# A graph network's second table kept by position: plain stores in place of scatters, and positions found ahead of the first table

## The chip, the core and the metric

The kernel runs on one core of one Trainium2 chip. The metric is the device time of one execution in microseconds (us), lower is better; the median of the runs is compared.

## What is computed

Two layers of a typed graph transformer over 6250 nodes of 128 features, 200000 edges sorted by destination, 32 relations (edge types) and 16 node types, then a dense layer and a normalised residual:

```python
def gt_layer(x, ntype, etype, src, dst, ...):        # 8 heads of 16
    k, q, v = (typed_linear(x, ntype, W) for W in (Wk, Wq, Wv))
    kT = jnp.einsum('nhd,htdo->nhto', k, Watt)       # one row per node and relation
    vT = jnp.einsum('nhd,htdo->nhto', v, Wmsg)
    kw, m = kT[src, :, etype], vT[src, :, etype]     # gathered per edge
    a = jnp.einsum('ehd,ehd->eh', kw, q[dst]) * pri[:, etype].T / SQRT_D
    att = edge_softmax(a, dst, n)
    hag = segment_sum((m * att[:, :, None]).reshape(-1, 128), dst, n)
    h = silu(typed_linear(hag, ntype, Wa))
    alpha = sigmoid(skip[ntype])[:, None]
    return layernorm(h * alpha + x * (1 - alpha)) * g + b
h = x
for l in range(2): h = gt_layer(h, ...)
return layernorm(x + (h @ ff_w + ff_b))
```

## The kernel before

The nodes are padded to 6272, 49 tiles of 128. For each layer a table in DRAM holds a row of 256 words (kT and vT, 1 KB) for every node and relation, 6272 x 32 rows, 205.5 MB. POOL then gathers, for each tile of 128 destinations, one row per edge and destination: a gather (line 887) is one indirect DMA that brings 128 rows, one per partition, into a slot of a ring of SBUF. There are 1613 gathers a layer. To keep that number small, destinations are sorted by their number of edges: a node's *position* is its place in that sorted list, tiles are made of neighbouring positions, and a tile takes as many slots as its largest destination has edges.

**First stretch.** Typed k and v columns are made by groups of two tiles (`one_typed`: masks on DVE at line 424, matmuls at 439), multiplied by the relations' weights (`table_rows`: matmul 472, emptied to one of four stages `sts` by ACT or DVE at 481), and sent to table 0 by SP (`send`, line 835, two DMAs of 1 MB for half a tile, 196 in all). The first three groups (`AHEAD`) come before a branch (`tc.If`) that would sort the edges if they weren't sorted. Beside this, `prepare` finds each destination's first edge with 50 gathers (535), its degree, and its position: a comparison with all bins (584, `hot`), counts by matmul (597 to 599, `total` and `ahead`), a running sum (602), a subtraction, an addition and a product (604 to 608), and a sum over bins (611, `pos_f`). From the positions follow `rec` (which node stands at a position), the x rows in order of position (663, 668) and the list `idx_all` of table rows by slot (673).

**Layer 0.** `gathers` issues on POOL; `attend` works on DVE with the slots that have landed, in pieces of up to 16 slots: product with the query (908), sum per head (910), softmax, product with the values (935), sum over slots (939). The rest of a group of tiles (four, at the end 3, 2, 2, 1, 1) runs in one *lane*: output map and norm (`behind`), then k and v of the next layer (`project`), then rows of table 1 (`next_tables`, again line 472 and 481) in two stages. A row of table 1 belongs to a node, tiles stand by position, so `scatter` (1129) writes each half tile, 2 MB, by an indirect DMA of POOL with the list `half`; 98 in all. A scatter stands in POOL's order among the gathers, `MARGIN` after its stage is planned to be full.

**Layer 1.** 1613 gathers from table 1 with the same `idx_all`, attention, and the output by 49 scatters.

**What sets the order.** Each engine runs its instructions in program order. The order is written by a planner: generators yield an engine, an estimated time and what they need, `plan.spawn` gives them a rank, and the planner emits the instruction that can start soonest by its estimates.

## Time and profile before

| what | us |
|---|---|
| median of 3 runs (lowest, highest) | 5355.41 (5348.28, 5358.69) |
| the profiled execution, its own time | 5361.82 |
| its span in the trace | 5360.0 |
| first stretch, to the first gather of layer 0 | 802.78 |
| layer 0, first to last gather | 802.78 to 3043.32 |
| layer 1, first gather | 3147.81 |
| busy: DVE, POOL, PE (TensorE matmul), ACT | 3876.2, 3552.9, 2562.4, 919.8 |

Times in rows are us from the start of the span unless marked ns. A row of windows gives the stretch, its length, the busy us (and count) of PE, PEld (weight loads), DVE, ACT and POOL, then TensorE's mean granted clock as a share of full speed, the share of time in which the 16 DMA engines were busy, and GB/s. In a timeline "[0.30 <-issue]" is the idle time of the engine ahead of the instruction and what ended it; "issue" is time in which it waited for nothing that the profile shows. A row of groups gives line, engine, operation, names out<-in, shapes and count, then the busy us and mean ns, then the idle time ahead of the group's instructions by what ended it. SPq is SP's queue: the us there is the time in which a DMA was being issued. DVE is VectorE, ACT ScalarE, POOL GpSimd, SP SyncE.

### The profile page before, as it was taken

The page shows a single profiled execution, that of the slowest core. Times are in us where ns is not written, and L with a number is a line of the kernel's source. Part 1 is how long each engine was busy: PE and PEld are TensorE (multiplying, and loading weights), DVE is VectorE, ACT ScalarE, POOL GpSimd, SP SyncE. Part 2 cuts the span into 40 slices and gives each one's busy share as a digit, 9 for nine tenths or more (in the row PEclk, how much of TensorE's full clock was granted, in tenths as well). Part 3 has the DMA queues.
Part 4 walks back from the last instruction along what each step waited for, and adds up shares of the span by engine and source line. Part 5 has one row for each costly group of instructions (what it writes and reads, how often), then busy time and mean ns, then how long its engine had stood idle before and what let it go on. Part 6 is the DMA issues. An engine that isn't in the chain of part 4 may idle for free. (4 is left out here: it accounts for less than half of the span.)

```text
span 5360.0 us, 35414 instructions
## 1 busy us (share of the span) xinstructions
PE 2562.4 (48%) x8598; PEld 1357.9 (25%) x8598; DVE 3876.2 (72%) x5522; ACT 919.8 (17%) x1814; POOL 3552.9 (66%) x3543
## 2 busy tenths in 40 slices
PE   6889972164755656565667841212213321221113
PEld 4455541022322322232334520101101111110002
DVE  5776755687787778777788826777777777776777
ACT  2233430011212211222223410000000000000001
POOL 0402306777777777777777547777777777777775
PEclk8899996576776667667777765656656655655556
DMA  6669985345646645655656643333333333333332
GB/s 243 261 250 390 365 330 129 106 151 179 207 142 206 221 146 186 223 196 183 203 198 240 239 167 114 108 115 114 116 106 114 115 110 105 112 110 108 109 102 76
DMA packets 323823, 923.80 MB, mean 172 GB/s; under 512 B 82896, under 2 KB 169932, under 8 KB 285976
## 3 DMA queue, kind: packets, MB, share of 16 engines
q0 software_dynamic: 176864, 645.82, 37.6%
q1 hardware_dynamic: 146744, 275.67, 14.2%
q8 instruction: 68, 1.11, 0.1%
q14 instruction: 147, 1.20, 0.1%
HBM read 488.51 MB, written 432.74 MB: 172 GB/s over the span
## 5 line engine op out<-in xcount | busy, mean ns | idle before, releaser
L887 POOL DMA_INDIRECT ring<-table,idx_all x3226 | 3240.8, 1005 | 1211.3 <-issue 970.0
L908 DVE TENSOR_TENSOR ring<-ring,sb 128x2048 f32<-128x2048 f32 (+13 forms) x261 | 453.8, 1739 | 728.1 <-DMA ring<-table,idx_all 709.1
L481 ACT COPY st<-tab 128x512 f32<-128x512 f32 x1175 | 614.2, 598 | 860.4 <-PE tab L472 437.7
L939 DVE TENSOR_REDUCE add<-ring 128x128 f32<-128x2048 f32 (+13 forms) x269 | 731.6, 2720 | 7.9
L1007 DVE SCALAR_TENSOR_TENSOR xm<-types,xb 128x512 f32<-128x512 f32 (+3 forms) x880 | 485.6, 588 | 103.5 <-PE av L1015 91.3
L472 PE MATMUL tab<-bv,vT 32*128 32x512 f32 x1568 | 405.1, 781 | 305.6 <-ACT st L481 303.9
L910 DVE TENSOR_REDUCE sb<-ring 128x128 f32<-128x2048 f32 (+13 forms) x269 | 472.9, 1758 | 7.0
L935 DVE TENSOR_TENSOR ring<-ring,sb 128x2048 f32<-128x2048 f32 (+13 forms) x269 | 469.4, 1745 | 0.0
L1015 PE MATMUL tab<-xm,wq 128*128 128x512 f32 (+3 forms) x416 | 215.6, 686 | 465.8 <-DVE xm L1007 465.8
L1015 PE MATMUL av<-xm,wa 128*128 128x512 f32 (+3 forms) x736 | 329.1, 610 | 201.5 <-DVE xm L1007 201.1
L481 DVE COPY st<-tab 128x512 f32<-128x512 f32 x393 | 256.3, 686 | 204.5 <-PE tab L472 137.3
L472 PE MATMUL tab<-bk,kT 32*128 32x512 f32 x1568 | 380.7, 780 | 25.4 <-ACT st L481 11.5
L1174 ACT COPY sb<-qr 128x128 f32<-128x128 f32 x96 | 25.9, 270 | 1849.9 <-DVE sb L910 1681.5
L1015 PE MATMUL av<-xm,wq 128*128 128x512 f32 (+3 forms) x544 | 237.2, 589 | 128.4 <-DVE xm L1007 126.3
L439 PE MATMUL kv<-xm,wk 128*128 128x256 f32 (+1 forms) x800 | 261.3, 409 | 63.1 <-DVE xm L424 63.0
L472 PEld LDWEIGHTS tab<-bv,vT 32*128 32x128 f32 x1568 | 174.2, 219 | 451.0 <-ACT st L481 401.6
L1015 PEld LDWEIGHTS av<-xm,wa 128*128 128x128 f32 x736 | 156.5, 230 | 369.2 <-DVE xm L1007 244.0
L1015 PEld LDWEIGHTS tab<-xm,wq 128*128 128x128 f32 x416 | 101.1, 269 | 568.3 <-DVE xm L1007 508.1
L439 PE MATMUL kv<-xm,wv 128*128 128x256 f32 (+1 forms) x800 | 243.2, 387 | 0.0
L1015 PE MATMUL ak<-xm,wk 128*128 128x512 f32 (+3 forms) x480 | 231.1, 566 | 24.8 <-DVE xm L1007 24.8
L1015 PE MATMUL av<-xm,wv 128*128 128x512 f32 (+3 forms) x480 | 222.0, 546 | 0.0
L1015 PE MATMUL tab<-xm,wa 128*128 128x512 f32 (+2 forms) x224 | 114.1, 672 | 178.6 <-DVE xm L1007 178.6
(207 smaller groups left out, 2917.1 us busy)
## 6 DMA issues: line engine op xcount, KB each, us to landing
table<-st SPq DMA_DIRECT2D x196, 1024.0 KB
ring<-table,idx_all POOLq DMA_INDIRECT x3226, 2.8
state<-init SPq DMA_DIRECT2D x2, 3528.0 KB
state<-state SPq DMA_DIRECT2D x98, 72.0 KB
types<-tyrow SPq DMA_DIRECT2D x20, 256.0 KB
rows<-in_x_dram SPq DMA_DIRECT2D x24, 128.0 KB
types_i<-in_node_type_dram SPq DMA_DIRECT2D x24, 128.0 KB
xperm<-xg SPq DMA_DIRECT2D x12, 256.0 KB
```

The costliest lines, as they stand in the source:

```text
L439: nc.tensor.matmul(to, w[:, t], xm, start=False, stop=last_of)
L472: nc.tensor.matmul(tab, cT[here, nodes], blk[here, t0 : t0 + per].rearrange("p t o -> p (t o)"), start=True, stop=True)
L481: (nc.scalar.copy if e == "ACT" else nc.vector.tensor_copy)(to, tab.rearrange("p (t o) -> p t o", o=width))
L887: nc.gpsimd.indirect_dma_start(out=ring[:, place], out_offset=None, in_=tables[layer], in_offset=bass.IndirectOffsetOnAxis(ap=idx[:, s : s ...
L908: nc.vector.tensor_tensor(kk, kk, q[:, None, :].to_broadcast([P, m, P]), op=ALU.mult)
L910: nc.vector.tensor_reduce(sc[:, s0 : s0 + m], kk.rearrange("p s (h d) -> p s h d", h=H), axis=AX.X, op=ALU.add)
L935: nc.vector.tensor_tensor(vv.rearrange("p s (h d) -> p s h d", h=H), vv.rearrange("p s (h d) -> p s h d", h=H), sc[:, s0 : s0 + m, :, None ...
L939: nc.vector.tensor_reduce(add, vv.rearrange("p s c -> p c s"), axis=AX.X, op=ALU.add)
L1007: nc.vector.scalar_tensor_tensor(xm[:, :M], types[:, :M], float(t), xT[:, :M], op0=ALU.is_equal, op1=ALU.mult)
L1015: nc.tensor.matmul(to[:, :M], w[:, t], xm[:, :M], start=(t == 0), stop=(t == NT - 1))
L1174: nc.scalar.copy(q, rows[0][:, j])
```

## The change

Table 1 is kept by position instead of by node. Its rows then lie in the order of the tiles, and SP stores each half tile by a plain DMA (`store`, line 1172 after); the list `half` and the scatters are gone. Layer 1 has to gather by position, so layer 0's table carries the place: its rows get a 257th word, 32 x position of the node + relation, added on DVE by `numbered`. In `attend` of layer 0, ACT copies that word of every landed slot over the slot's entry in `idx_all`. For that the positions must be known by node before any row of table 0 goes out: `pos_f` goes to DRAM (`posd`) and comes back turned, TensorE transposes it and DVE multiplies by 32 (`places`). So no table is made before the branch; typed columns run ahead and are kept for 11 groups (`KEPT`), the relations' weights are loaded late, the counts use five banks of PSUM instead of one, and the subtraction at 604 is folded into `upper`. A loop for more edges than slots, which runs no round with these edges, looks positions up by itself.

```diff
-AHEAD = 3
+AHEAD = 2
+KEPT = 11
+    WIDTH = [ROW + 1, ROW]
-    tables = [dtile(f"table{i}", [ROWS, ROW]) for i in range(L)]
+    tables = [dtile(f"table{i}", [ROWS, w]) for i, w in enumerate(WIDTH)]
+    posd = dtile("posd", [NP, 1])
...
+    def places(posn, got):
+        us = yield "PE", Work(P), [got]
+        to = tabs[0]
+        nc.tensor.transpose(to[:, :NTILE], posn, ident[:NTILE, :NTILE])
+        us = yield "DVE", 0.3, [us]
+        nc.vector.tensor_scalar(place32, to[:, :NTILE], float(RT), None, op0=ALU.mult)
+        known.us = us
...
-        nc.vector.tensor_scalar(upper, lanes, lane, None, op0=ALU.is_gt)
+        nc.vector.tensor_scalar(upper, lanes, lane, -1.0, op0=ALU.is_gt, op1=ALU.add)
+        counted = us
-                us = yield "PE", Work(112), [us]
-                n_ps = prep_bank()
+                us = yield "PE", Work(112), [counted]
+                n_ps = tabs[c0 // 448 % len(tabs)]
...
-        nc.vector.tensor_sub(upto, upto, total)
-        yield "DVE", dve_us(BT), ()
...
+        yield "SP", 0.4, [us]
+        nc.sync.dma_start(out=posd.rearrange("(p t) c -> p (t c)", t=NTILE), in_=pos_f)
+        got = yield "SP", 0.4, ()
+        posn = pp.tile([NTILE, P], F32, tag="posn")
+        nc.sync.dma_start(out=posn, in_=posd.rearrange("(t p) c -> t (p c)", p=P))
+        plan.spawn(places(posn, got + 5.0), RANK["prepare"])
...
-        if i > 1:
-            yield "SP", 0.0, [used[i - 2]]
-        kT, ks = yield from copied(ap, "kT", kv[:, :HALF], M, 2, [end])
+        if i >= KEPT:
+            yield "SP", 0.0, [used[i - KEPT]]
+        kT, ks = yield from copied(ap, "kT", kv[:, :HALF], M, KEPT, [end])
...
+    def relation_blocks():
+        us = yield "SP", 17.0, ()
+        relations.extend(load_relations(first, 0))
+        yield "DVE", 3.5, [us + 3.0]
+    def numbered(st, c, t, needs):
+        us = yield "DVE", 0.2, needs
+        nc.vector.tensor_scalar(st[:, :, ROW], kinds_r[:, c * RT // 2 :][:, : RT // 2], place32[:, t : t + 1], None, op0=ALU.add)
+        return us
     def first_tables(part):
+        yield "SP", 0.0, [known]
...
-        plan.spawn(first_tables(range(AHEAD)), RANK["table"], 8.0)
+        plan.spawn(relation_blocks(), RANK["late"], 25.0)
...
-        plan.spawn(first_tables(range(AHEAD, len(GROUPS))), RANK["table"])
+        plan.spawn(first_tables(range(len(GROUPS))), RANK["table"])
...
+            if after is not None:
+                done = yield "ACT", act_us(m), landed[s0 : s0 + m]
+                nc.scalar.copy(after[:, s0 : s0 + m], ring[:, r, ROW])
...
-    def scatter(t, c, rows, filled, done, margin, at):
-        us = yield "SP", 0.0, filled
-        us = yield "POOL", Issue(GATHER_US, STORE_US), [us + margin]
-        s = nc.gpsimd.indirect_dma_start(
-            out=tables[1].rearrange("(n t) c -> n (t c)", t=RT // 2),
-            out_offset=bass.IndirectOffsetOnAxis(ap=half[:, t, c : c + 1], axis=0), ...)
+    def store(t, c, rows, filled, done, at):
+        us = yield "SP", 0.8, filled
+        dest = tables[1][t * P * RT : (t + 1) * P * RT].rearrange("(p t) c -> p t c", t=RT)
+        nc.sync.dma_start(out=dest[:, c * RT // 2 :][:, : RT // 2], in_=rows)
```

POOL's order in layer 0, before, at one place (`table_60` is table 0, `table_61` table 1, `st` a stage; x9 is nine of them in a row):

```order
L1132 DMA table_61<-st_5709,half 12544x4096
L887 DMA ring<-table_60,idx_all 128x256 x9
L1132 DMA table_61<-st_5708,half 12544x4096
L887 DMA ring<-table_60,idx_all 128x256 x8
L1132 DMA table_61<-st_5709,half 12544x4096
L887 DMA ring<-table_60,idx_all 128x256 x8
L1132 DMA table_61<-st_5708,half 12544x4096
L887 DMA ring<-table_60,idx_all 128x256 x9
L1132 DMA table_61<-st_5709,half 12544x4096
```

And POOL's order after, from the last instruction of the first stretch's own (the branches between are the loop that runs no round) through layer 0:

```order
L914 DMA ring<-table_60,wi 128x257 x16
L998 REGISTER_ALU
L998 COMPARE_AND_BRANCH
L998 UNCONDITIONAL_BRANCH
L996 REGISTER_ALU
L996 COMPARE_AND_BRANCH
L996 UNCONDITIONAL_BRANCH
L914 DMA ring<-table_60,idx_all 128x257 x1613
L994 TENSOR_LOAD n_over
```

All 1613 gathers now stand in one row, where scatters stood between them.

SP's order around the branch (`L853` before, `L883` after), before:

```order
L769 DMA rows<-in_x_dram 128x2x128
L788 DMA types_i<-in_node_type_dram 128x256
L389 DMA csort<-comb 128x1564
L390 DMA csort<-pad 1x391
L835 DMA table_60<-st_112 128x2048 x2
L835 DMA table_60<-st_113 128x2048 x2
L835 DMA table_60<-st_114 128x2048 x2
...
L835 DMA table_60<-st_113 128x2048 x2
L835 DMA table_60<-st_114 128x2048 x2
L853 COMPARE_AND_BRANCH
L1389 COMPARE_AND_BRANCH
```

And after, from the last loads ahead of the first sends:

```order
L577 DMA nt_i<-in_node_type_dram 112x49
L578 DMA nt_i<-in_node_type_dram 15x49
L580 DMA nt_i<-in_node_type_dram 1x27
L789 DMA rows<-in_x_dram 128x2x128
L808 DMA types_i<-in_node_type_dram 128x256
L627 DMA posd<-pos_f 128x49
L630 DMA posn<-posd 49x128
L865 DMA table_60<-st_116 128x2056 x2
L865 DMA table_60<-st_117 128x2056 x2
L865 DMA table_60<-st_118 128x2056 x2
L789 DMA rows<-in_x_dram 128x2x128
L808 DMA types_i<-in_node_type_dram 128x256
```

The sends of table 0 (`L835`, now `L865`, 2056 words a partition for 2048) began ahead of the branch; they now stand behind the writing and reading back of the positions (`L627`, `L630`).

SP's order at the start of layer 0, before (loads of x rows, of types and of states, and stores of hidden rows and queries):

```order
L899 DMA state<-state_66 128x144 x4
L1051 DMA xs<-xperm 128x4x128
L1216 DMA types<-tyrow 128x512
L899 DMA state<-state_66 128x144
L1095 DMA hid<-h 128x4x128
L899 DMA state<-state_66 128x144
L1114 DMA qrows<-q 128x4x128
L899 DMA state<-state_66 128x144 x2
L1051 DMA xs<-xperm 128x4x128
L1216 DMA types<-tyrow 128x512
L899 DMA state<-state_66 128x144
L1095 DMA hid<-h 128x4x128
```

And after:

```order
L926 DMA state<-state_67 128x144 x4
L1092 DMA xs<-xperm 128x4x128
L1252 DMA types<-tyrow 128x512
L926 DMA state<-state_67 128x144
L1136 DMA hid<-h 128x4x128
L926 DMA state<-state_67 128x144
L1172 DMA table_61<-st_5797 128x4096
L1172 DMA table_61<-st_5798 128x4096
L1172 DMA table_61<-st_5797 128x4096
L1155 DMA qrows<-q 128x4x128
L1172 DMA table_61<-st_5798 128x4096
L926 DMA state<-state_67 128x144
```

The stores of table 1 (`L1172`) now stand among the loads of states (`L899`, now `L926`).

## Rows read from the trace of the kernel before

**Rows 1.** Windows by stage: busy us of each engine, clock, DMA share, GB/s.
```profile
802.00:3046.00 2244.00, 1288.87 (x3455) 630.06 (x3456) 1706.23 (x2174) 471.36 (x945) 1711.81 (x1703) 0.69 0.56 186
2800.00:3046.00 246.00, 197.10 (x706) 115.19 (x705) 202.85 (x349) 91.28 (x186) 188.66 (x188) 0.79 0.69 241
3046.00:3148.00 102.00, 65.05 (x352) 44.83 (x350) 44.38 (x115) 36.74 (x71) 7.94 (x9) 0.76 0.52 208
3148.00:5360.00 2212.00, 529.55 (x1223) 268.66 (x1223) 1584.34 (x2097) 151.49 (x298) 1669.15 (x1662) 0.59 0.37 108
```

**Rows 2.** Timeline of POOL: start, us, instruction, idle time before it.
```profile
802.78 1.01 POOL L887 DMA_INDIRECT ring<-table,idx_all  x1 [198.96 <-DVE low L965]
804.10 1.00 POOL L887 DMA_INDIRECT ring<-table,idx_all  x1 [0.30 <-issue]
...
3043.32 1.00 POOL L887 DMA_INDIRECT ring<-table,idx_all  x1 [0.30 <-issue]
...
3129.14 0.97 POOL L1132 DMA_INDIRECT table<-st,half  x1 [7.44 <-DMA table<-st,half]
3147.81 1.06 POOL L887 DMA_INDIRECT ring<-table,idx_all  x1 [17.71 <-issue]
```

**Rows 3.** Groups of POOL's instructions in layer 0, 802 to 3046.
```profile
L887 POOL DMA_INDIRECT ring<-table,idx_all x1613 | 1620.7, 1005 | 702.6 <-issue 473.2 <-DVE low L965 199.0 <-DVE add L939 12.2
L1132 POOL DMA_INDIRECT table<-st,half x90 | 91.1, 1012 | 27.4 <-issue 21.9 <-ACT st L481 5.2 <-DMA ring<-table,idx_all 0.3
```

**Rows 4.** Waits of DVE in the same stage: us in total, times, longest.
```profile
DVE ring L908 <- DMA ring<-table,idx_all: 253.0, 63, 17.7
```

**Rows 5.** Windows of the first stretch, from the first send on.
```profile
69.00:400.00 331.00, 281.03 (x1525) 177.40 (x1524) 252.87 (x466) 105.76 (x206) 71.71 (x73) 0.91 0.72 278
400.00:500.00 100.00, 97.20 (x502) 56.59 (x499) 62.56 (x128) 36.12 (x69) 25.53 (x26) 0.97 1.04 402
500.00:600.00 100.00, 96.65 (x502) 57.27 (x501) 73.91 (x237) 37.28 (x72) 62.88 (x62) 0.98 0.98 385
600.00:700.00 100.00, 99.33 (x510) 56.30 (x508) 70.22 (x143) 42.64 (x84) 3.16 (x4) 1.00 0.83 330
700.00:803.00 103.00, 75.57 (x436) 46.14 (x432) 55.63 (x115) 34.10 (x64) 0.22 (x1) 0.89 0.83 333
```

**Rows 6.** Line L1132 from 802 to 2975: durations and first and last start.
```profile
L1132 POOL DMA_INDIRECT table<-st,half x84: 1009/1010/1152, 1173.9 to 2969.9; - x84
```

**Rows 7.** Groups of ACT's instructions in layer 0, 802 to 3046.
```profile
L481 ACT COPY st<-tab 128x512 f32<-128x512 f32 x681 | 351.4, 601 | 517.7 <-DMA table<-st,half 394.4 <-PE tab L472 122.9
...
L1174 ACT COPY sb<-qr 128x128 f32<-128x128 f32 x48 | 13.0, 270 | 456.6 <-DVE sb L910 419.3 <-DVE ring L935 21.5 <-DVE top L917 14.1
```

**Rows 8.** Timelines of SP, POOL and DVE in the first stretch.
```profile
21.26 8.55 SPq L313 DMA_DIRECT2D bk<-in_L_gnn_Watt_dram  x8
...
34.08 3.72 SPq L325 DMA_DIRECT2D pr<-in_L_gnn_pri_dram  x8
...
68.91 18.75 SPq L835 DMA_DIRECT2D table<-st  x8
...
126.17 0.19 POOL L501 IOTA nid<- 128x50 f32 x1 [124.83 <-DMA table<-st]
...
46.16 0.14 DVE L381 CAST flag<-pb 1x1 int32<-1x1 f32 x1
...
249.26 3.43 DVE L584 TENSOR_TENSOR hot<-bin__1711,bins 128x3136 bf16<-128x3136 f32 x1
...
290.54 6.68 DVE L602 TENSOR_TENSOR_SCAN upto<-total 128x3136 f32<-128x3136 f32 x1
297.25 3.42 DVE L604 TENSOR_TENSOR upto<-upto,total 128x3136 f32<-128x3136 f32 x1
...
307.70 5.71 DVE L611 TENSOR_REDUCE pos_f<-upto 128x49 f32<-128x3136 f32 x1
...
791.46 0.91 DVE L310 MEMSET bk<- 128x1024 f32 x1 [14.33 <-DMA table<-st]
```

More of the change, by code (lines that the diff above doesn't have):

```diff
@@ L490, in gnn_kernel @@
     ov = ctile("ov", [P, NTILE, 2], I32)
-    placed = When()
+    placed, known = When(), When()
+    place32 = first.tile([P, NTILE], F32, tag="place32", name="place32")
+    kinds_r = first.tile([P, RT], F32, tag="kinds_r", name="kinds_r")
+    nc.gpsimd.iota(kinds_r, pattern=[[1, RT]], base=0, channel_multiplier=0, allow_small_or_imprecise_dtypes=True)
     def prep_bank():
         return ps.tile([P, GT * P], F32, tag="pb", name="pb")
+    def places(posn, got):
[5 more added lines that the diff above has]
+        known.us = us
     def prepare():
@@ L750, in apart @@
         on_pool[0] = s.ins
-    sts = [first.tile([P, RT // 2, ROW], F32, tag=f"st{c}", name=f"st{c}") for c in range(STAGES)]
+    sts = [first.tile([P, RT // 2, ROW + 1], F32, tag=f"st{c}", name=f"st{c}") for c in range(STAGES)]
     made = [When() for _ in GROUPS]
@@ L803, in one_typed @@
             made[i - 1] if i else 0.0, [us])
[L804 to L807 removed]
+        if i >= KEPT:
+            yield "SP", 0.0, [used[i - KEPT]]
+        kT, ks = yield from copied(ap, "kT", kv[:, :HALF], M, KEPT, [end])
+        vT, vs = yield from copied(ap, "vT", kv[:, HALF:], M, KEPT, [end])
         columns[i] = kT, vT
@@ L810, in gnn_kernel @@
     free, relations = [0.0] * STAGES, []
+    def relation_blocks():
[6 more added lines that the diff above has]
+        return us
     def first_tables(part):
-        if not relations:
-            us = yield "SP", 17.0, ()
-            relations.extend(load_relations(first, 0))
-            yield "DVE", 3.5, [us + 3.0]
+        yield "SP", 0.0, [known]
         bk, bv = relations
@@ L827, in first_tables @@
                 for c, u in enumerate(use):
+                    us = yield from numbered(sts[u], c, t, [free[u]])
+                    halves[c].append(us)
                     free[u] = When()
@@ L877, in gnn_kernel @@
     low = ctile("low", [P, NTILE, 2], I32)
-    half = ctile("half", [P, NTILE, 2], I32)
-    for c in range(2):
-        nc.vector.tensor_scalar(half[:, :, c], rec[:, :, 2], 2.0, float(c), op0=ALU.mult, op1=ALU.add)
     bp = ctx.enter_context(tc.tile_pool(name="bp", bufs=2))
@@ L893, in heads, with attend @@
         return t.rearrange("p (h d) -> p h d", h=H)
-    def attend(ring, pieces, pen, n, q, before, acc, landed, free, needs, read):
+    def attend(ring, pieces, pen, n, q, before, acc, landed, free, needs, read, after=None):
         got = yield "SP", 0.4, ()
@@ L932, in attend @@
             m = r.stop - r.start
-            vv = ring[:, r, P:]
+            vv = ring[:, r, P:ROW]
             yield "DVE", dve_us(m * P), ()
@@ L986, in attend_over @@
                 query_rows(fp, layer, n0, q)
+                if layer:
+                    node = bp.tile([P, ROUND], I32, tag="node", name="node")
+                    nc.vector.tensor_scalar(node, wi, RT.bit_length() - 1, None, op0=ALU.logical_shift_right)
+                    nc.vector.tensor_scalar(wi, wi, RT - 1, None, op0=ALU.bitwise_and)
+                    at = bp.tile([P, ROUND], F32, tag="at", name="at")
+                    for i in range(ROUND):
+                        nc.gpsimd.indirect_dma_start(
+                            out=at[:, i : i + 1], out_offset=None, in_=posd,
+                            in_offset=bass.IndirectOffsetOnAxis(ap=node[:, i : i + 1], axis=0),
+                            bounds_check=NP - 1, oob_is_err=False)
+                    nc.vector.scalar_tensor_tensor(wi, at, float(RT), wi, op0=ALU.mult, op1=ALU.add)
                 for i in range(ROUND):
@@ L1123, in next_tables @@
             for c in range(2):
[L1124 to L1125 removed]
+                plan.spawn(store(t, c, at["rows"][c], halves[c], at["st"][c], at), RANK["table"])
         at["read"][i].us = plan.free["PE"]
         locks["s"].give(plan.free["PE"])
[L1129 to L1136 removed]
+    def store(t, c, rows, filled, done, at):
+        us = yield "SP", 0.8, filled
+        dest = tables[1][t * P * RT : (t + 1) * P * RT].rearrange("(p t) c -> p t c", t=RT)
+        nc.sync.dma_start(out=dest[:, c * RT // 2 :][:, : RT // 2], in_=rows)
         done.us = at["dma"] = max(us, at["dma"]) + 7.5
@@ L1298, in attends @@
                                            states[layer][t * P : (t + 1) * P], hag[:, j], landed[span], free, [ready[t]],
-                                           read[t])
+                                           read[t], None if layer else idx_all[:, span])
                 past[t].us = plan.free["DVE"]
@@ L1315, in gnn_kernel @@
             size = RINGS[layer]
-            ring = rp.tile([P, size, ROW], F32, tag="ring", name="ring")
+            ring = rp.tile([P, size, WIDTH[layer]], F32, tag="ring", name="ring")
             wqs.append(load_typed(wp, "wq0", Wq[layer]))
```

8 lines of the change are left out of this document (1 added, 7 removed).

## The prediction

> **What bounds the kernel now.** I first cut the profiled execution into its stages by what each engine does in them [rows 1]. The table of layer 1 is complete and layer 0 over at 3148; the stage from 802 to 3046 is the one that the change rebuilds. POOL is busy for 1711.81 of its 2244 us, DVE for 1706.23, PE for 1288.87, and the DMA share is 0.56. That looks like a tie of POOL and DVE, so the second view is POOL's own timeline [rows 2]: each gather takes 1.00 us, and 0.30 us of "issue" stands ahead of the next one, in which POOL waits for nothing that the profile shows. The groups of instructions say the same of all 1613 gathers: 1005 ns each, 473.2 us of idle time put down to issue, and only 12.2 us to DVE [rows 3]. So POOL is full: one indirect DMA per 1.005 + 473.2/1553 = 1.31 us, whatever it moves. 1613 gathers and 90 scatters at 1.31 make 2231 us, and from the first gather at 802.78 to the last at 3043.32 are 2240.5 [rows 2]. The third view is DVE's list of waits: DVE waited 253.0 us, 63 times, for gathered rows [rows 4]. DVE is the one that waits, POOL the one that is waited for. In layer 0 the path is POOL; a scatter there costs what a gather costs.
>
> After the last gather the path leaves POOL: attention of the last tiles, their next-layer columns, and the last table rows run one after another until layer 1's first gather at 3147.81, 104.5 us later [rows 2]. In the first stretch it is another pair: TensorE is busy 96 to 99% from 400 to 700, and the DMA share is 1.04 and 0.98 from 400 to 600 [rows 5]. Layer 1 (from 3148) issues the same 1613 gathers before and after; only the values of the indices differ, so I count it at nothing.
>
> **Part 1: the scatters leave POOL.** 90 of the 98 scatters lie among the gathers of layer 0, 84 of them before the last gather of the third tile from the end, at 2975 [rows 6]. Each holds POOL for one slot, so that tile's rows are there 84 x 1.31 = 110 us sooner. I don't count the other 14: the last three tiles go through one lane one after another, and the lane is then the path (POOL has 9 instructions in the 102 us from 3046 to 3148, PE is busy 65.05 [rows 1]).
>
> What is late next? DVE: 1706 us of work would have to fit in 2244 - 110, 80% instead of 76%. It fits. In the last 246 us it is tighter: 202.85 us of DVE work [rows 1], and 18 scatters fewer there would leave 246 - 24 = 222 us, 91%. Attention and the lane share DVE, so part of those 24 us can come back as queueing. Ends: 0 and 24; I take 10, a little under the middle, since DVE is still not full.
>
> The store itself: SP issues the same 2 MB that POOL issued, so the bytes don't change. In the tail the last scatter started after 7.44 us of waiting for the one before it to land [rows 2]; stores of separate rows needn't do that, and two landings overlap. I give it 3 us, between 0 and 7.4. The new wait is SP's: a store waits for its stage to be filled, and behind it in SP's order stand the loads of states, types and x rows for the next tiles. Before, it was POOL where such a wait stood, and POOL was idle for 27.4 us ahead of its 90 scatters [rows 3]. SP has nothing else to do, and the loads are issued a tile ahead, so I take 0 and keep 27 for the range.
>
> New work in layer 0: for every piece of 16 slots or fewer ACT casts one word per slot into the index list. The nearest row is ACT's copy of 128 elements, 270 ns [rows 7]; some 135 pieces (a mean of 12 slots in 1613) make at most 36 us on an engine that worked 471.36 us of 2244 [rows 1]. The cast waits for the gathered rows, and table emptying (L481) stands behind it on ACT; but that waits already, 394.4 us of it for scatters to land [rows 7], where the store frees its stage without POOL's queue. Nothing for the sum. Rows of 1028 instead of 1024 bytes add 0.4% to a DMA share of 0.56: hidden.
>
> Layer 0 and tail: -110 + 10 - 3 = **-103**, between -113 (-110 - 3, nothing returned) and -60 (24 returned by DVE, 27 by SP, no gain of 3).
>
> **Part 2: the first stretch turns round.** The place in the second table must be in the row of the first, so no row of table 0 may go out before the positions are known. Before, the first send started at 68.91, and positions were ready at 307.70 + 5.71 = 313.4 [rows 8]. When are they ready after? Before, the search began at 126.17, when POOL had waited 124.83 us for table sends at the branch; none are out at the branch now. The flag that the branch reads was made at 46.16 [rows 8]; I take the search's start at 48. From 126.17 to 313.4 the chain took 187.2. It loses the subtraction, 3.42 (297.25 to 300.7). The 14 counts, which ran one by one through one bank between 249.26 + 3.43 and 290.54, 37.9 us, now use several banks; the ends are 8.4 (14 copies at ACT's 0.60 for 512 elements [rows 7]) and 37.9, and I take 17, nearer to the copies because masks and copies of other work stand between, so -21. Against that the weights of the relations, from 21.26 to 34.08 + 3.72 = 37.8 on SP [rows 8], 16.5 us, are now loaded just behind the branch, and DVE stands before them: +16, between 0 and 30. Writing the positions out, reading them back transposed, and the first filled stage: +14, between 8 and 20. So the first send: 48 + 187 - 3 - 21 + 16 + 14 = **241**, instead of 69, between 215 and 265.
>
> Then all of table 0 has to go out: 6272 x 32 rows of 1028 bytes are 206.3 MB. The whole of 69 to 803 moved 278 x 331 + 402 x 100 + 385 x 100 + 330 x 100 + 333 x 103 = 238 MB before [rows 5], of which 205.5 are table rows; of the other 32.5 about half (edge search, edge loads) is over by 241. So 223 MB remain. TensorE has meanwhile done typed columns, which are now kept for 11 groups instead of 2, so for the first part of the rest tables are there to be sent as fast as DMA takes them. Rate: the two windows with a full DMA share show 402 and 385 GB/s, 600 to 803, where TensorE is the limit, 330 and 333 [rows 5]. I take 385, the window in which gathers of index lists run beside the sends, as they will: 223/0.385 = 579 us, the end at 820. Before, the last table rows had landed at 791.46 [rows 8]. So layer 0 starts **+29** us later; ends: -18 (215 and 402 GB/s: 215 + 555 = 770, -21, less the 3 us that setup before the first gather may add) and +67 (265 and 376). What follows the positions on POOL (x rows, index lists: over by 600 before, with POOL idle 198.96 us before the first gather [rows 2]) has room. The 98 additions of the place, 128 x 16 words each, are less than the 270 ns of 128 elements [rows 7]: under 26 us on a DVE that is 54 to 76% busy [rows 5]; nothing.
>
> [...]
>
> **Rivals.** (a) Layer 0 gives more back: the lane and DVE together lose the ends above, so the gain is 60 instead of 103. For it: 91% DVE in the last window. Against: DVE's 253 us of waits. Time: 5361.8 + 29 - 60 - 6.4 = 5324.
> (b) The first stretch is no longer than before: known early and 402 GB/s, -15. Time 5361.8 - 15 - 103 - 6.4 = 5237. Against it: the late start.
> (c) Slower: TensorE, not DMA, sets the pace after the positions are known, because in its fixed order the typed columns of the last groups stand between tables, and a table that waits for a stage holds them up. It ran at 331 GB/s there before; all of the rest at this rate is 223/0.331 = 674, the end 915, +124. Time 5361.8 + 124 - 103 - 6.4 = 5376. It decides from +103 on, 241 + 223/rate over 894, below 341 GB/s. Against it: 7 groups' columns are done by then, work that TensorE shared with tables before.
> (d) Rows that start anywhere cost DMA time. The two windows with a full share differ by 4% (402 and 385 [rows 5]); one more such step, 370, makes 223/0.370 = 603, 24 more than 579; in layer 0 a share of 0.56 stays under 1 even at half as much time again for every byte. Time 5282 + 24 = 5306. [...]
> (e) POOL doesn't speed up because gathers now wait for ring slots: 12.2 us of such a wait exist now [rows 3]. With DVE at the rate of 1706 in 2134 that would need an attention that falls behind for a whole ring of 64; then the 103 are not gained, 5361.8 + 29 - 6.4 = 5384, but I see nothing for it.
>
> **How the numbers follow.** 5361.8 (own time of the profiled execution; its span is 5360.0) + 29 - 103 = 5288; the runs' median, 5355.4, lies 6.4 below that execution, so **5282**. Chances: forecast 0.54 (5240 to 5315), (a) 0.17, (b) 0.14, (c) 0.07, (d) 0.06, (e) 0.02. The range of 8 in 10 is 5235 to 5340: it takes in (a), (b) nearly and (d), and leaves out (c) and (e). About 0.2%, 11 us, is what a measurement can tell from no change here. Faster: 0.54 + 0.14 + 0.06 + 0.13 of (a) = 0.87; within 0.2%: 0.04 of (a) and 0.02 of (c), 0.06; slower 0.07.
>
> **What would show it.** POOL in layer 0 with 1613 indirect DMAs and no other, still one per 1.31, DVE's wait for gathers down to some 140 us; the first send near 241 and DMA share about 1.0 from there to about 820; first gather at about 832, the first gather of layer 1 at about 3074; layer 1 of 2212 us as now. Wrong if DMA has holes between 241 and 820 while TensorE is full (c), if gathers show idle time for DVE (e), if the tail after the last gather is much over 104 us (a), or if layer 1 changes.

## The result: 30 us of the 73 that were forecast

The changed kernel takes 5318.69 us (median of 5 runs, 5314.55 to 5327.44); the kernel before takes 5348.86 (median of 5, 5347.81 to 5358.69). The ratio is 0.994, with a 95% interval of 0.9925 to 0.9954: faster, clear of noise, by 30 us. The forecast was 5282, with a gain of 73 against the median of 5355.41 known then. The time lies in the range of 5235 to 5340, but the gain is less than half of the forecast one.

The two profiled executions are compared stage by stage. The one of before took 5361.82 us, 13 more than the later median; the one of after took 5318.69, its median. So 43 us separate the traces, and the medians 30.

| stage | before, us | after, us | difference | forecast |
|---|---|---|---|---|
| first stretch, to the first gather of layer 0 | 802.78 | 865.51 | +62.7 | +29 |
| layer 0, first to last gather | 2240.5 | 2121.5 | -119.0 | |
| tail, to the first gather of layer 1 | 104.5 | 120.2 | +15.7 | |
| layer 0 and tail together | 2345.0 | 2241.7 | -103.3 | -103 |
| layer 1 and the end of the span | 2212.2 | 2209.7 | -2.5 | 0 |

Layer 0 and its tail came out as forecast, the first stretch didn't.

POOL's timeline of the kernel after (start us, us, engine, line, operation, idle time before it), which answers to [rows 2]:

```profile
865.51 1.01 POOL L914 DMA_INDIRECT ring<-table,idx_all  x1 [303.35 <-DVE low L995]
...
2987.06 1.00 POOL L914 DMA_INDIRECT ring<-table,idx_all  x1 [0.30 <-issue]
3107.24 0.99 POOL L914 DMA_INDIRECT ring<-table,idx_all  x1 [119.18 <-issue]
```

Its group of gathers in layer 0 (866 to 2990), answering to [rows 3], then DVE's wait for gathers, answering to [rows 4], then ACT's groups of table emptying, answering to [rows 7], and of casts, which are new:

```profile
L914 POOL DMA_INDIRECT ring<-table,idx_all x1613 | 1615.6, 1002 | 810.3 <-issue 479.5 <-DVE low L995 303.3 <-DMA ring<-table,idx_all 5.5
```

```profile
DVE ring L938 <- DMA ring<-table,idx_all: 200.5, 45, 17.1
```

```profile
L484 ACT COPY st<-tab 128x512 f32<-128x512 f32 x675 | 349.7, 599 | 198.2 <-PE tab L475 147.9 <-DMA table<-st 46.8 <-PE xb L414 2.7
L934 ACT CAST idx_all<-ring 128x16 int32<-128x16 f32 (+13 forms) x135 | 28.9, 216 | 903.9 <-DMA ring<-table,idx_all 896.5 <-issue 7.2
```

POOL does 1613 indirect DMAs instead of 1703, each as long as before (1002 ns, 1005 in [rows 3]), and 90 x 1.31 = 118 us are gone. DVE still waits 200.5 us for rows (253.0 before; some 140 were expected), so POOL is still what layer 0 goes by. ACT's wait for stages to land fell from 394.4 us to 46.8, now that no store stands in POOL's queue. The casts keep ACT busy for 28.9 us.

Now the first stretch: windows of the kernel after, ahead of the first send (below it the same window of the kernel before) and from it to the landing of the last table row at 854 (columns as in [rows 5]), then the start of the search for positions, the bins, the running sum, the positions, the first send, and the wait for the last landing:

```profile
0.00:243.00 243.00, 156.19 (x768) 120.81 (x768) 163.85 (x270) 15.42 (x31) 70.34 (x71) 0.82 0.31 82
```

```profile
0.00:243.00 243.00, 172.02 (x915) 107.44 (x916) 153.80 (x254) 55.61 (x105) 64.22 (x70) 0.86 0.71 253
```

```profile
243.00:300.00 57.00, 57.00 (x318) 35.66 (x318) 45.18 (x122) 22.89 (x44) 0.00 (x0) 1.00 0.88 351
300.00:400.00 100.00, 87.15 (x441) 51.66 (x440) 60.24 (x146) 32.57 (x63) 16.13 (x17) 0.91 0.98 357
400.00:500.00 100.00, 97.43 (x493) 57.13 (x497) 66.34 (x151) 35.95 (x67) 36.05 (x37) 0.98 1.01 400
500.00:600.00 100.00, 95.04 (x473) 50.26 (x465) 75.15 (x239) 46.27 (x89) 48.43 (x47) 0.98 0.93 368
600.00:700.00 100.00, 94.82 (x470) 52.79 (x470) 66.57 (x147) 36.92 (x72) 0.00 (x0) 0.95 0.83 334
700.00:800.00 100.00, 97.41 (x510) 58.91 (x509) 68.20 (x149) 44.46 (x81) 0.00 (x0) 0.91 0.92 378
800.00:854.00 54.00, 35.03 (x118) 18.10 (x111) 20.66 (x38) 16.55 (x30) 0.00 (x0) 0.56 0.96 397
```

```profile
40.14 0.19 POOL L516 IOTA nid<- 128x50 f32 x1 [38.74 <-DMA bk<-in_L_gnn_Watt_dram]
...
187.07 3.43 DVE L599 TENSOR_TENSOR hot<-bin__1343,bins 128x3136 bf16<-128x3136 f32 x1
...
206.29 6.68 DVE L618 TENSOR_TENSOR_SCAN upto<-total 128x3136 f32<-128x3136 f32 x1
...
220.00 5.71 DVE L625 TENSOR_REDUCE pos_f<-upto 128x49 f32<-128x3136 f32 x1
...
242.90 13.04 SPq L865 DMA_DIRECT2D table<-st  x6
...
854.06 0.91 DVE L313 MEMSET bk<- 128x1024 f32 x1 [16.68 <-DMA table<-st]
```

The windows from 243 to 854 add up to 225 MB, 2 more than reckoned, and the first send stands at 242.9 for a forecast 241. What differs is the rate: 225 MB in 611 us are 368 GB/s, not 385. In those 611 us TensorE is busy for 563.88 (92%), and where the DMA share falls, as to 0.83 from 600 to 700, TensorE is at 95%. Its last table matmul starts at 835.6, 18 us ahead of the last landing; in the kernel before these are 775.8 and 791.46, 16 us. So the sends end right behind TensorE's last tables.

Ahead of 243 it is the other way round: TensorE works 156.19 of 243 us. The kernel before, which made tables too in that time, had 172.02 there. The typed columns that were to be made ahead were made for seven of the 25 groups, and the rest had to be made among the tables. That is a reading; the experiments test it. What TensorE waited for longest up to 243 were masks from DVE, which also does the edge search in that time (us in total, times, longest):

```profile
PE kv L442 <- DVE xm L427: 35.2, 11, 15.4
```

In five of the study's seven groups of runs the kernel before took 6264 to 6318 us, and every kernel that was run in both kinds of groups was some 900 to 1140 us longer there; these numbers are marked "longer condition" and compared only with each other.

### The profile page after: what moved, and what is told of

It reads as the page before. It is cut to its first block, busy times and chain, and to the rows that moved or that the text cites. A ratio compares the mean times of both kernels' runs of the same rounds, so it can differ in the third digit from the quotient of the medians.

```text
span 5316.9 us, 36038 instructions
## 1 busy us (share of the span) xinstructions
PE 2575.6 (48%) x8599; PEld 1371.0 (26%) x8599; DVE 3924.0 (74%) x5652; ACT 930.8 (18%) x1917; POOL 3451.2 (65%) x3446
## 5 line engine op out<-in xcount | busy, mean ns | idle before, releaser
L969 DVE TENSOR_REDUCE add<-ring 128x128 f32<-128x2048 f32 (+13 forms) x269 | 749.5, 2786 | 7.8
L484 ACT COPY st<-tab 128x512 f32<-128x512 f32 x1138 | 601.3, 597 | 574.0 <-PE tab L475 454.5
L475 PE MATMUL tab<-bv,vT 32*128 32x512 f32 x1568 | 429.5, 804 | 113.1 <-ACT st L484 108.5
L475 PE MATMUL tab<-bk,kT 32*128 32x512 f32 x1568 | 408.9, 788 | 71.9 <-ACT st L484 56.2
L484 DVE COPY st<-tab 128x512 f32<-128x512 f32 x430 | 280.1, 686 | 210.5 <-PE tab L475 167.7
L475 PEld LDWEIGHTS tab<-bk,kT 32*128 32x128 f32 x1568 | 166.6, 220 | 197.1 <-ACT st L484 114.4
```

Source lines behind the costliest of these rows:

```text
L475: nc.tensor.matmul(tab, cT[here, nodes], blk[here, t0 : t0 + per].rearrange("p t o -> p (t o)"), start=True, stop=True)
L484: (nc.scalar.copy if e == "ACT" else nc.vector.tensor_copy)(to, tab.rearrange("p (t o) -> p t o", o=width))
L969: nc.vector.tensor_reduce(add, vv.rearrange("p s c -> p c s"), axis=AX.X, op=ALU.add)
```

## Experiments

**The changed kernel again.** Its start (first gather at 864.6), its layer 0 (2126.0 us, tail 122.7) and the ratio repeat within 7 us.

> The changed kernel as it is, beside the kernel before on the same chip. The runs of this study so far were on chips on which the kernel before takes some 6265 us, with ACT and TensorE standing still for up to 74 us at a time with nothing that the profile names; the first result was taken where it takes 5349. If a chip like the first comes: 0.994 of the kernel before, first gather at 865, first gather of layer 1 at 3107. If one like the others comes: theory A holds first gather +60 to +65 against the kernel before; and as layer 0 is there not set by POOL (POOL waited 282 us for DVE and 276 us for filled stages in it), the plain store brings nothing, and the whole is 60 to 190 us slower than before (e3_first_only +60, e2_store_only +126).

Measured 5329.31 us beside 5361.81 (0.9939, 0.9916 to 0.9961): the first case of the two. The changed kernel itself has no run under the longer condition.

**The store alone, in the kernel before.** Layer 1 gathers rows of other nodes, as many and as large.

```diff
-    half = ctile("half", [P, NTILE, 2], I32)
...
-                plan.spawn(scatter(t, c, at["rows"][c], halves[c], at["st"][c], MARGIN if i + 2 < NG else 0.0, at),
-                           RANK["table"])
+                plan.spawn(store(t, c, at["rows"][c], halves[c], at["st"][c], at), RANK["table"])
...
+    def store(t, c, rows, filled, done, at):
...
+        nc.sync.dma_start(out=dest[:, c * RT // 2 :][:, : RT // 2], in_=rows)
```

> The store of table 1 by plain DMA alone, in the kernel before, once more where that kernel takes 5350 to 5360 us (layer 1 gathers rows of other nodes, as many and as large). Theory A: first gather at 803, last gather of layer 0 about 2122 us after it instead of 2240, the tail some 15 us longer, first gather of layer 1 about 103 us sooner, the whole 103 us (1.9%) shorter. Rival C (casts and wide rows took part of the gain): 115 or more.

Measured 5253.85 us beside 5353.46: ratio 0.9817 (0.98 to 0.9833), 100 us less. POOL's timeline:

```profile
804.74 1.01 POOL L884 DMA_INDIRECT ring<-table,idx_all  x1 [199.31 <-DVE low L962]
...
2926.44 1.00 POOL L884 DMA_INDIRECT ring<-table,idx_all  x1 [0.30 <-issue]
3043.12 1.00 POOL L884 DMA_INDIRECT ring<-table,idx_all  x1 [115.69 <-issue]
```

The first gather is within 2 us of where it was, layer 0 takes 2121.7 us and the tail 116.7. That is theory A; rival C (casts and wide rows took part of the gain) falls, since with them layer 0 takes 2121.5. The tail is 12 us longer than before here, 16 in the changed kernel; no run shows why.

**The first stretch alone.** The changed kernel with the scatters put back and no casts.

```diff
-                plan.spawn(store(t, c, at["rows"][c], halves[c], at["st"][c], at), RANK["table"])
+                plan.spawn(scatter(t, c, at["rows"][c], halves[c], at["st"][c], MARGIN if i + 2 < NG else 0.0, at),
+                           RANK["table"])
...
-                                           read[t], None if layer else idx_all[:, span])
+                                           read[t], None)
```

> The changed kernel with the other part alone: positions ahead of table rows and rows of 257 words, but table 1 by node with POOL's scatters as before, and no casts of the index list. Theory A: first gather at about 865 (63 us later than before), layer 0 and its tail of 2345 us as before, the whole 5349 + 60 = 5409. Rival C: if the later first gather is partly due to something that is not of the first stretch, or layer 0 is slower with wide rows, it is off by over 10 us from that.

> Positions ahead of table rows and rows of 257 words alone, with POOL's scatters and no casts, once more. Theory A: first gather at 865, the rest as before, the whole 60 to 63 us longer (1.2%).

The first ran under the longer condition: 60 us more, 1.0093 (1.006 to 1.0127). The second measured 5424.16 us: 1.0131 (1.0114 to 1.0148), 71 us more, 8 above the 60 to 63 that were expected. POOL's timeline:

```profile
869.69 1.01 POOL L917 DMA_INDIRECT ring<-table,idx_all  x1 [304.20 <-DVE low L998]
...
3109.86 1.00 POOL L917 DMA_INDIRECT ring<-table,idx_all  x1 [0.30 <-DMA table<-st,half]
...
3216.45 1.05 POOL L917 DMA_INDIRECT ring<-table,idx_all  x1 [17.64 <-issue]
```

Layer 0 takes 2240.2 us and the tail 106.6, much as before (2240.5 and 104.5); the first gather is 67 us later than before, 4 later than in the changed kernel, which no run explains. The two parts add up: -100 + 71 = -29, and the whole change gives -30.

**Wide rows alone, in the kernel before.**

```diff
+    WIDTH = [ROW + 1, ROW]
...
-    tables = [dtile(f"table{i}", [ROWS, ROW]) for i in range(L)]
+    tables = [dtile(f"table{i}", [ROWS, w]) for i, w in enumerate(WIDTH)]
...
-    sts = [first.tile([P, RT // 2, ROW], F32, tag=f"st{c}", name=f"st{c}") for c in range(STAGES)]
+    sts = [first.tile([P, RT // 2, ROW + 1], F32, tag=f"st{c}", name=f"st{c}") for c in range(STAGES)]
+    for s in sts:
+        nc.vector.memset(s[:, :, ROW], 0.0)
...
-            ring = rp.tile([P, size, ROW], F32, tag="ring", name="ring")
+            ring = rp.tile([P, size, WIDTH[layer]], F32, tag="ring", name="ring")
```

> The kernel before, with the rows of table 0 made 257 words wide in DRAM, in the four stages and in layer 0's ring; the 257th word is a zero that nobody reads. Nothing else moves. Theory A (TensorE is what runs short in the changed first stretch; the width of a row costs only its 0.4% of bytes): first gather of layer 0 at 803 to 807 instead of 802.8, one gather per 1.31 us as before, whole time +0 to +6 us. [...]

> Rows of 257 words alone in the kernel before, once more. Theory A: first gather 803 to 807, whole +0 to +6 us. Theory B (unaligned rows slow the DMA engines by some 5% where they are full): first gather 10 to 25 us later, whole +10 to +30.

Measured 5357.41 us: 1.0007 (0.9997 to 1.0017), 4 us more and not clear of noise; first gather at 808.43. The windows with a full DMA share, beside 402 and 385 GB/s of [rows 5]:

```profile
400.00:500.00 100.00, 96.22 (x497) 56.04 (x496) 62.53 (x128) 36.12 (x68) 23.88 (x24) 0.97 1.05 398
500.00:600.00 100.00, 95.41 (x486) 56.10 (x487) 71.36 (x230) 35.45 (x67) 61.30 (x61) 0.97 0.97 383
```

1% less, not 5: theory B, the prediction's rival (d), falls. In layer 0, where DMA isn't full, its share is 0.59 for 0.56 before at the same 186 GB/s, so some price can't be excluded there; it is hidden. Under the longer condition (e1_wide_rows) the ratio was 1.0011 (0.9985 to 1.0038).

**Half of the typed work taken away.** The changed kernel without v's typed matmuls in the first stretch; v's columns are copied from k's.

```diff
-            ap, "xm", xT, tf, M, [(wk, kv[:, :HALF]), (wv, kv[:, HALF:])], [], [kv], (1,),
+            ap, "xm", xT, tf, M, [(wk, kv[:, :HALF])], [], [kv], (0,),
-        vT, vs = yield from copied(ap, "vT", kv[:, HALF:], M, KEPT, [end])
+        vT, vs = yield from copied(ap, "vT", kv[:, :HALF], M, KEPT, [end])
```

> The changed kernel without the typed matmuls of v in the first stretch (v's columns are copied from k's, so the values are wrong); TensorE loses about half of its typed work there, some 170 us, DMA nothing. Theory A (TensorE short after the positions are known): sends end when 223 MB at 385 to 402 GB/s have gone, 555 to 580 us after the first send instead of 611, so first gather 30 to 55 us sooner than 865, and the DMA share stays at 0.95 to 1.0 from 500 to 800. Theory B (DMA slow by its rows): 611 us stay 611, first gather within 10 us of 865.

> The changed kernel without the typed matmuls of v in the first stretch (v's columns are copied from k's, so the values are wrong), once more, since on the chip of the first four runs every kernel was some 900 us longer, the one before too. Theory A (TensorE short after the positions are known): 555 to 580 us from the first send to the last landing instead of 611, first gather 30 to 55 us sooner than 865. Theory B (DMA slow by its rows): 611 us stay, first gather within 10 us of 865.

> The changed kernel without v's typed matmuls in the first stretch (values wrong), once more. Theory A (TensorE short after the positions are known): 555 to 580 us from the first send to the last landing instead of 611, first gather 30 to 55 us sooner than 865. Theory B (DMA slow by its rows): 611 us stay, first gather within 10 us of 865.

The last one measured 5277.87 us (0.9861, 0.9841 to 0.9881), 41 us less than the changed kernel, 35 of them at the first gather. Windows from the first send on, then the first send, the last landing and the first gather:

```profile
237.00:300.00 63.00, 62.90 (x324) 32.50 (x326) 56.73 (x148) 30.67 (x59) 0.00 (x0) 1.00 1.01 414
300.00:400.00 100.00, 79.47 (x361) 40.69 (x354) 61.44 (x153) 32.38 (x62) 12.21 (x13) 0.86 1.03 379
400.00:500.00 100.00, 95.72 (x452) 51.06 (x450) 70.27 (x171) 39.04 (x77) 36.00 (x36) 1.00 1.03 405
500.00:600.00 100.00, 81.43 (x339) 38.56 (x339) 70.31 (x236) 40.91 (x79) 51.98 (x51) 0.80 0.92 357
600.00:700.00 100.00, 91.28 (x415) 45.64 (x417) 72.33 (x160) 47.71 (x92) 0.00 (x0) 0.83 0.91 373
700.00:800.00 100.00, 100.00 (x311) 51.99 (x309) 52.18 (x97) 42.87 (x78) 0.00 (x0) 0.50 1.01 418
```

```profile
236.19 3.46 SPq L865 DMA_DIRECT2D table<-st  x4
...
818.05 0.91 DVE L313 MEMSET bk<- 128x1024 f32 x1 [16.68 <-DMA table<-st]
...
830.08 1.01 POOL L914 DMA_INDIRECT ring<-table,idx_all  x1 [256.57 <-DVE low L995]
```

582 us for 225 MB, 386 GB/s, where the prediction had 579 us and 385. So 385 was a rate that DMA reaches, with rows of 1028 bytes too (418 GB/s from 700 to 800), and TensorE kept the changed kernel 29 us from it (611 - 582). The other 7 of the 35 us at the first gather come from the earlier first send. The DMA share wasn't full throughout, though that was expected: it is 0.92 and 0.91 from 500 to 700, where TensorE stood idle for 27 us, waiting for masks from DVE (16.5) and for a row that ACT empties (10.5). So even here the order ahead of the tables costs something. The same kernel under the longer condition (e5_half_typed, e5b_half_typed) has its first gather at 876.9 and 873.2 where the first stretch of the change alone has 916.9: 40 to 44 us.

**Tables that don't wait.** The changed kernel with the place set to zero from the start and the casts written to a list that nobody reads, so that layer 1 gathers rows of other nodes. Everything else of the change is done.

```diff
+    known.us = 0.0
...
+    nc.vector.memset(place32, 0.0)
...
-        nc.vector.tensor_scalar(place32, to[:, :NTILE], float(RT), None, op0=ALU.mult)
-        known.us = us
+        other32 = pp.tile([P, NTILE], F32, tag="other32", name="other32")
+        nc.vector.tensor_scalar(other32, to[:, :NTILE], float(RT), None, op0=ALU.mult)
...
-                nc.scalar.copy(after[:, s0 : s0 + m], ring[:, r, ROW])
+                spare = bp.tile([P, 16], I32, tag="spare", name="spare")
+                nc.scalar.copy(spare[:, :m], ring[:, r, ROW])
```

> The changed kernel with tables that don't wait for the positions: the place added is zero from the start, and the casts go to a list that nobody reads (so layer 1 gathers rows of other nodes, as many and as large). All other work of the change is there. Theory A (the moment of the positions costs all of the first stretch's loss): first send before 90, first gather at 803 to 812, the whole as e2b_store_only, 5254 to 5265. Rival D (the additional work of the change, 98 additions, 130 casts, other order, costs a part): first gather over 815, or the whole over 5270.

> The changed kernel with tables that don't wait for the positions (place zero, casts to a list that nobody reads), once more. Theory A: first gather at 803 to 812, the whole like e2b_store_only, 100 us less than the kernel before, within 12. Rival D (additions, casts and other order of the change cost a part): first gather over 815, or the whole over 5270.

> The changed kernel with tables that don't wait for the positions (place zero, casts to a list that nobody reads), once more. Theory A: first gather at 803 to 812, the whole 100 us less than the kernel before, within 12. Rival D (additions, casts and other order of the change cost a part): first gather over 815, or the whole less than 85 us shorter.

It ran three times, each under the longer condition, with whole times of 6412.12 to 6472.68, 1.0212 to 1.0263 of the kernel before; the 100 us less that were expected didn't come, as they don't for the store alone under this condition. Only its first stretch can be judged. First send at 77 to 78, first gathers at 866.9, 869.6 and 870.2; under the same condition the kernels with tables ahead of the branch have 867.9 (e1_wide_rows) and 864.5 (e2_store_only), and e3_first_only has 916.9:

```profile
870.19 1.01 POOL L916 DMA_INDIRECT ring<-table,idx_all  x1 [282.17 <-DVE low L998]
```

So the 98 additions (18.6 us of DVE in the changed kernel), the kept columns and the other order cost the first stretch no more than a few us; that tables wait for the positions costs the rest, 47 to 50 us here. This comparison has a weakness: in every trace of the longer condition the first stretch loses time in one place, where from 500 to 600 TensorE has 178 to 317 matmuls and DMA moves 180 to 259 GB/s (473 and 368 in the changed kernel). First gathers under it are compared as if that loss were the same in each. The whole time where the kernel before takes 5350 stays unmeasured.

**Weights later.** Four attempts at winning some back; all ran under the longer condition, so they are judged by their first gathers. The first moves the relations' weights behind the branch's plan.

```diff
-        plan.spawn(relation_blocks(), RANK["late"], 25.0)     # plan ahead of the branch
...
+        plan.spawn(relation_blocks(), RANK["late"], 120.0)    # plan behind it
```

> The changed kernel with the relations' weights loaded in the second plan from its 120 us on instead of ahead of the branch's end, so that DVE does not stand before them (and before the masks behind them) while the search waits from 42 to 71. Theory A: positions 15 to 25 us earlier, first send at about 220, and about as much sooner the last landing while DMA and TensorE are both nearly full behind it: the whole 10 to 25 us shorter than the changed kernel, 5295 to 5310 where that takes 5320. If typed columns made ahead are what counts: fewer of them are made by then, and the gain is under 10.

Whole 6463.82 (1.028), first gather at 912.04, first send at 243.95 where about 220 was expected. DVE's timeline has the reason, beside the same instruction in the changed kernel:

```profile
151.92 0.18 DVE L329 TENSOR_SCALAR pr<-pr 128x32 f32<-128x32 f32 x1 [15.35 <-DMA pr<-in_L_gnn_pri_dram]
```

```profile
51.90 0.18 DVE L329 TENSOR_SCALAR pr<-pr 128x32 f32<-128x32 f32 x1 [9.29 <-DMA pr<-in_L_gnn_pri_dram]
```

The search for edge blocks ended 15 us sooner (86.6 for 101.4), but then DVE stood 15.35 us before the same load, among the edge counts. The wait was moved, not removed.

**States early, and a second bank.** Both build on the last one.

```diff
-            yield "SP", 5.5, [placed]
+            yield "SP", 5.5, ()            # e9: initial states, spawned at 60
...
+        at = tabs[4] if i in (3, 5) else kv    # e7: two groups in a bank of their own
```

> As e4_weights_late, and the initial states (2 x 3528 KB, 35 us of SP between 325 and 344 in the changed kernel, with TensorE waiting 13 us for stages beside them) written ahead of the positions, when the DMA share is 0.2 and less. Theory A with DMA as the limit: 7 MB less at 385 GB/s, another 10 to 20 us shorter than e4_weights_late. Theory A with TensorE as the only limit: within 5 us of e4_weights_late.

> As e4_weights_late, and typed columns of groups 3 and 5 accumulated in a bank of their own, so that TensorE need not wait for the copies of the group before (14.2 us in one such wait). Theory A: some 15 us more of typed work done by the first send, 5 to 15 us shorter than e4_weights_late. If TensorE's gaps there are set by DVE's masks instead: within 5 us of e4_weights_late.

First gathers at 906.12 and 914.58 (whole 6461.22 and 6461.18). With one trace each, the states' 7 MB ahead of the positions give 6 us, between the two cases expected, and the second bank nothing (TensorE's busy time to 243 is 151.84 us there, 149.45 in e4): the copies between groups weren't what held the typed columns. Whether DVE's masks do, the longest wait shown above, no run tests.

**Scaling late, states early.** The weights' loads stay ahead, only DVE's scaling of them moves behind the edge search, and the states go out at about 92.

```diff
     def relation_blocks():            # loads alone, as early as before
...
+    def relation_scale():             # spawned at 150 in the second plan
+        yield "DVE", 1.6, ()
+        bk, bv, pr = relations
+        nc.vector.tensor_scalar(pr, pr, float(HS) ** -0.5, None, op0=ALU.mult)
+        nc.vector.tensor_tensor(bk, bk, pr[:, :, None].to_broadcast(list(bk.shape)), op=ALU.mult)
```

> The changed kernel with the weights' loads left where they are, but DVE's scaling of them moved behind the edge search (so that DVE neither stands before the loads at 42 to 71 nor at 136), and the initial states written at about 110, when DMA has little to do. Theory A: first send 10 to 20 us earlier, at 223 to 233; 7 MB less behind it, 10 to 18 us; first gather 15 to 35 us sooner than the changed kernel (865 where the kernel before takes 5350 to 5360), and the whole as much shorter, 5285 to 5305. If the search is held by something else (TensorE's typed work and the masks before it): first send at 240 or later, and only the states' gain, 5 to 18 us.

> As e10_both (DVE's scaling of the weights behind the edge search, initial states at about 110), once more. Theory A: first send at 225 to 233 instead of 243, first gather at 825 to 845 instead of 865, the rest unchanged, the whole 20 to 40 us shorter than the changed kernel, 50 to 75 us less than the kernel before. If only the moment of the first send counts: 12 us.

Both ran under the longer condition. First send at 230.9 and 231.6, TensorE busy for 164.80 and 166.48 us to 243, first gathers at 874.8 and 877.4:

```profile
877.39 1.01 POOL L924 DMA_INDIRECT ring<-table,idx_all  x1 [344.28 <-DVE low L1005]
```

That is 34 to 42 us sooner than e3_first_only, e4 and e7 have it there (912 to 917). So most of the first stretch's loss (47 to 50 us there) was won back. The first send is 11 to 15 us earlier and the states gave about 6 in e9, which is half of it; more typed work isn't done by then (757 matmuls of TensorE up to the first send, 759 to 767 in the other three), it is done sooner. What gave the rest isn't shown. Whether the whole beats the changed kernel where that takes 5320 isn't shown: the whole times, 6462.91 and 6480.71 (1.0253 and 1.0248), are of the other condition, and the changed kernel itself has no run there.

**What the longer condition says of layer 0.** 

> The kernel before with one part of the change: table 1 stored by position with plain SP DMAs, no scatter on POOL. The indices are not changed, so layer 1 gathers rows of other nodes than it should (the same number of gathers of the same size). Theory A (the gain of layer 0 is the POOL slots of the scatters, and all of the loss is in the first stretch): first gather at 803 as before, last gather of layer 0 about 2240 - 118 = 2122 us after it, first gather of layer 1 about 103 us sooner than before, the whole 5349 - 103 = 5246. Rival C (the casts and the wide rows of the changed kernel took part of the gain away again, so the store alone gives more): below 5235.

Under that condition the store alone was not faster but slower: 6395.51 us beside 6269.54, 1.0185 (1.0158 to 1.0212). POOL's waits in layer 0, of e1_wide_rows (scatters) and then of e2_store_only (stores), and ACT's longest in e1:

```profile
POOL table L1135 <- ACT st L482: 304.4, 36, 28.1
POOL ring L890 <- DVE add L942: 282.3, 13, 47.7
```

```profile
POOL ring L884 <- DVE add L936: 731.3, 40, 44.8
```

```profile
ACT yT L1025 <- remote: 854.9, 15, 115.9
```

A gather still costs 1.31 us, but POOL waits for ring slots and for stages; in the same stretch ACT stands still for up to 116 us at a time and TensorE for up to 74, with no cause that the trace names. POOL isn't the path there, and its freed slots turn into waiting. Why the store then loses 126 us instead of nothing (layer 0 66 us longer and the tail 41 than in e1) isn't settled; a candidate, not tried, is that loads stand behind stores on SP.

## Why the prediction came out as it did

**What bounds the kernel, and part 1 (scatters): right.** POOL's slot price gave -118 for all 90 scatters, and layer 0 is 119.0 shorter; the tail is 15.7 longer. The prediction counted 84 scatters, -110, which leaves +6.7 for what it put at +10 - 3. The mechanism (a scatter costs POOL what a gather costs, 1012 and 1005 ns in [rows 3], and at the end the lanes decide: in the tail POOL waits 119.18 us ahead of layer 1's first gather) holds. That the sum comes out at -103.3 for -103 is partly luck: the 10 was picked between 0 and 24. Casts and wide rows cost layer 0 nothing (2121.5 us with them, 2121.7 without). One sign that it named didn't show: DVE's wait for gathers is 200.5 us, not some 140.

**Part 2, the first send: right in the sum.** 241 forecast, 242.9 measured. Its parts are off and cancel, which is luck: the search begins at 40 instead of 48, takes 147 us to the bins instead of 139, the counts 16 instead of 17 (190.5 to 206.3), and from the positions to the first send it is 17 instead of 14.

**Part 2, the rate: the step that failed.** "TensorE has meanwhile done typed columns ... so for the first part of the rest tables are there to be sent as fast as DMA takes them", and 385 GB/s. The trace of before had the number that speaks against it: windows with TensorE at 97 to 99% [rows 5]. Tables and typed columns were already as much work as the stretch had time for, and 243 us of typed work alone used TensorE for only 156. The term was 579 us; with TensorE relieved it measured 582, with TensorE as it is 611, of which 5 are the 2 MB more. Of the 34 us by which the first stretch was missed, 32 are this term and 2 the first send. A part of TensorE's shortage may be its clock, which the prediction left out: as many matmuls up to the first gather (3571, before 3570) kept it busy for 720 us at a mean granted clock of 0.88, and for 679 at 0.92 before. No run separates this from the columns that were missing.

**Rivals.** (c), TensorE sets the pace, was the right mechanism at a third of its size: 368 GB/s, not 331, and it was put at 7%. (d), unaligned rows, put at 370 GB/s and 5306 us, would have looked much the same, and is refuted for the first stretch by e1b: with rows of 1028 bytes the two windows with a full DMA share show 398 and 383 GB/s, beside 402 and 385 without, 1% less at most. (a) and (b) didn't happen; (e), gathers waiting for ring slots, is what the longer condition shows, and not this result.

**The offset.** The prediction took the profiled execution of before to be 6.4 us above the median and carried this over; that of after lay at its median. So the 37 us between 5282 and 5318.69 are 34 of the first stretch and 6 of this offset, less 3 of layer 1 and the end. Of the 43 us that the gain is short, 31 are the stages, and the rest is that the profiled execution of before lay 13 above the later median.

## To carry to other kernels

Putting a transfer behind a result turned a stretch that hid work into two here: one in which TensorE idled and one in which everything was due at once. Reckon the second one by every engine that was nearly full before, not by the transfer's own rate alone. Where freed slots of one engine are to shorten a stage, its wait list says whether that engine is the path; under the longer condition, where POOL wasn't, the same store gained nothing and the kernel was 126 us slower.

## What the runs showed that was not expected

Rows of 1028 bytes instead of 1024 cost 0.07% (-0.03 to +0.17) of the kernel before: 398 and 383 GB/s for 402 and 385. The DMA share of layer 0 rose with them, from 0.56 to 0.59, without a price in time. And the longer condition came to the same kernels with gathers as short as ever (1.00 us) and ACT and TensorE standing still between instructions; its cause stays open.
